# Attention scores from hi/lo pairs, query products over 512 weight columns, and buffer rings of other lengths, in a two-layer transformer kernel

## The chip, the cores and the metric

The kernel runs on one core of a Trainium2 chip, in one launch. The metric is the device time of that launch in microseconds; three runs of the kernel before gave 2274.55, 2277.7 and 2279.82 us, a median of 2277.7 us. Of the core's engines the text speaks of TensorE (PE: matrix products, with weight loads as instructions of their own, PEld), VectorE (DVE), ScalarE (ACT), GpSimd (POOL) and the SyncE queue that issues transfers (SP). Matrix products write to eight PSUM banks of 128 partitions by 512 float32 each; everything else lives in SBUF.

## The reference

Sixteen batches of 64 tokens, width 512, go through two layers. Each sublayer adds its result to x and normalizes over the last axis:

```
x = ln(x + L0_attn(x))      # 32 query heads, 8 kv heads of 128, causal
x = ln(x + L0_xattn(x))     # linear attention over channels, 8 heads of 64
x = ln(x + L0_ffn(x))       # int4 weights with scales, silu(gate) * up, down
x = ln(x + L1_attn(x))      # 32 query heads, 8 kv heads, ALiBi bias
x = ln(x + L1_xattn(x))     # q and k over their rms; keys and values from the context
x = ln(x + L1_ffn(x))       # base plus gated low-rank experts
```

The three softmax attentions share one form, and it is the part that the change is about:

```
q = x @ wq; k, v = src @ wk, src @ wv       # L1_xattn: q = rms(q) * qnw, k = rms(k) * knw
s = (q . k) / sqrt(128) + mask
o = softmax(s) @ v;  out = o @ wo
```

Each kv head serves four query heads (a group). All inputs are float32 and the result is float32.

## The kernel before

A float32 matrix is used on TensorE as a pair hi + lo of fp32r matrices (hi is the value rounded to fp32r, lo the exact rest), and a product is three products, hi*hi + hi*lo + lo*hi, added up in one PSUM bank: `mm3`, lines 101 to 107. The pair is made by a ScalarE copy (hi) and a subtraction (lo), which is VectorE's work where the source lies in PSUM (`split_ps`, lines 91 and 92) and GpSimd's where it lies in SBUF (`split_sb`, lines 86 and 87). Weights come in pieces of 128x512 float32 (256 KB) over the SP queue into tiles `st`, and are split from there.

`Stream` (lines 828 to 1013) runs an attention as steps: one step is one kv head and four batches, 32 steps for a layer, 96 in all. A step has the following parts.

- `scores` (line 847), which is issued two steps ahead, multiplies queries and keys: for each of four batches and two pairs of query heads one product of 128 query rows by 64 keys, straight in float32 (line 856). Both operands are plain float32 tiles: `qt`, the transposed queries of a head and half of the tokens ([hd, 8 batches, 256], 8 KB per partition, two buffers), and `kt`, the transposed keys ([hd, 512], two buffers). Then follow the softmax on VectorE, ScalarE and GpSimd, and the tile `p` with hi and lo of the probabilities side by side.
- `pt` transposes `p` (line 878), `av` multiplies by V (line 889) and splits the result into a tile `ot`, and `oproj` multiplies the previous step's `ot` by the output weights (`mm3`) and adds to x (line 904).
- Between them stand the projections for later heads, in six parts a head (`half_units`, line 817): in the two self attentions `k_unit` and four `q_unit`s, each 12 products of 512 columns into a bank `mm` (of which there are two), evacuated by one ScalarE copy (lines 777 and 788). In the cross attention `qn_front` (line 790) makes the queries of a token tile token-major, with the 128x128 slices of x as the stationary operand, in two groups of 12 products of 256 weight columns each; `rms` divides by the root mean square; `qn_back` transposes (line 807) and copies to `qt` (line 809). The cross attention's keys are loaded by `k_unit` from a scratch tensor `ktd` in DRAM.
- `v_unit` (line 811) computes V of a token tile and `store_v` (line 147) splits it into two tiles `v` and writes them to DRAM; `load_vs` reads them back by batch.

`kv_stream` (line 165) fills `ktd` and the context's V during L0's ffn: `back` transposes the normalized keys into a bank, ScalarE scales them into `pts` (line 186), and one transfer writes them. `q_stream` (line 359) is the queries' side of the linear attention, in chunks of 128 that go through five stages, one a tick (`logits`, `exp`, `norm`, `transpose`, `out`), its work tiles being taken from the tags `s`, `p` and `le`. `l0_ffn` (line 440) keeps the inner activations of two items in one tile `qt`.

The order of instructions on each engine is set by a scheduler when the program is built: it follows the order of the code, moves instructions past each other where one would wait, and takes the softmax and the evacuations marked by `soon` (line 74) early. Buffers are rings by tag, of the lengths in `BUFS` (line 34) and `BANKS` (line 35); a write into a ring's oldest buffer waits for the last reader of it.

## Time and profile before

The profile is of one execution. The page gives its span from the first to the last instruction, 2275.4 us, and no time of its own beside it; the span is 2.3 us below the median of the three timed runs and within their spread.

| what | value |
|---|---|
| median of three runs | 2277.7 us (2274.55 to 2279.82) |
| span of the profiled execution | 2275.4 us |
| PE busy | 2208.5 us (97%), 13200 products |
| PEld busy | 1917.7 us (84%), 13200 loads |
| DVE busy | 1346.0 us (59%), 2523 instructions |
| ACT busy | 1124.1 us (49%), 2195 |
| POOL busy | 1172.9 us (52%), 1001 |
| DMA | 267.24 MB, 117 GB/s on average |
| granted TensorE clock | 0.994 |

Busy times are unions of intervals, so for pipelined products the duration of one (from its start to its modelled end) is longer than the distance to the next; the distance between starts in the timeline is what a product costs in a stream of products. A float32 product that is not a transposition appears as two records (two passes), each with its own weight load; an fp32r product appears as one.

The stages by time: L0 attention from the start to about 750 us, with the linear attention's two sides beside it; L0 ffn, the rest of the linear attention and `kv_stream` to about 1150; L1 self attention to about 1650; L1 cross attention to about 2240; the last L1 ffn tiles to the end.

### The profile page before, as it was taken

The page shows a single profiled execution, that of the slowest core. Times are in us where ns is not written, and L with a number is a line of the kernel's source. Part 1 is how long each engine was busy: PE and PEld are TensorE (multiplying, and loading weights), DVE is VectorE, ACT ScalarE, POOL GpSimd, SP SyncE. Part 2 cuts the span into 40 slices and gives each one's busy share as a digit, 9 for nine tenths or more (in the row PEclk, how much of TensorE's full clock was granted, in tenths as well). Part 3 has the DMA queues.
Part 4 walks back from the last instruction along what each step waited for, and adds up shares of the span by engine and source line. Part 5 has one row for each costly group of instructions (what it writes and reads, how often), then busy time and mean ns, then how long its engine had stood idle before and what let it go on. Part 6 is the DMA issues. An engine that isn't in the chain of part 4 may idle for free.

```text
span 2275.4 us, 36680 instructions
## 1 busy us (share of the span) xinstructions
PE 2208.5 (97%) x13200; PEld 1917.7 (84%) x13200; DVE 1346.0 (59%) x2523; ACT 1124.1 (49%) x2195; POOL 1172.9 (52%) x1001
## 2 busy tenths in 40 slices
PE   8999999999999999999999999999999999999998
PEld 7888888888888777777788888888898899988996
DVE  3655555667645789887743343433356566666656
ACT  5665556555444455555444444444444454443442
POOL 3533334455554655464654554545455666554641
PEclk9999999999999999999999999999999999999999
DMA  7533333322334322456543443334333343332320
GB/s 231 158 115 109 112 105 120 110 84 77 91 114 154 120 83 86 153 180 184 156 144 106 131 126 119 116 111 140 107 113 101 115 123 99 103 105 85 112 70 29
DMA packets 255317, 267.24 MB, mean 117 GB/s; under 512 B 32672, under 2 KB 168352, under 8 KB 255136
## 3 DMA queue, kind: packets, MB, share of 16 engines
q1 hardware_dynamic: 255136, 264.90, 38.1%
q8 instruction: 105, 1.72, 0.3%
q14 instruction: 76, 0.62, 0.1%
HBM read 231.26 MB, written 33.55 MB: 116 GB/s over the span
## 4 chain that ended last, share of the span: by engine, by line
PE 79%; DMA 5%; DVE 5%; POOL 5%; issue 2%; ACT 2%; SPq 0%; POOLq 0%; DVEq 0%; ACTq 0%
PE mm L105 16%; PE mm L106 15%; PE mm L107 15%; PE sc L856 6%; PE o L889 4%; PE fx L105 3%; PE fx L107 3%; PE fx L106 3%; PE pt L878 2%; DMA st<-in_down_s 1%; POOL wo L87 1%; PE fx L325 1%; POOL wq L87 1%; PE fx L298 1%; PE fx L316 1%
## 5 line engine op out<-in xcount | busy, mean ns | idle before, releaser
L87 POOL TENSOR_TENSOR wq<-st,wq 128x512 fp32r<-128x512 f32 x200 | 263.7, 1331 | 329.2 <-ACT wq L86 326.1
L107 PE MATMUL mm<-wo,ot 128*128 128x512 f32 x896 | 352.2, 393 | 0.0
L87 POOL TENSOR_TENSOR wo<-st,wo 128x512 fp32r<-128x512 f32 x226 | 296.6, 1342 | 96.8 <-ACT wo L86 88.0
L105 PE MATMUL mm<-wo,ot 128*128 128x512 f32 x768 | 315.2, 410 | 3.4 <-DVE x L904 3.1
L904 DVE TENSOR_TENSOR x<-x,mm 128x512 f32<-128x512 f32 x192 | 131.1, 683 | 308.2 <-PE mm L107 307.8
L106 PE MATMUL mm<-wo,ot 128*128 128x512 f32 x768 | 301.1, 392 | 0.0
L105 PE MATMUL mm<-xth,wq 128*128 128x512 f32 x512 | 204.9, 400 | 0.6 <-DVE v L92 0.3
L106 PE MATMUL mm<-xtl,wq 128*128 128x512 f32 x512 | 200.9, 392 | 0.0
L107 PE MATMUL mm<-xth,wq 128*128 128x512 f32 x512 | 200.6, 392 | 0.0
L107 PEld LDWEIGHTS mm<-wo,ot 128*128 128x128 f32 x896 | 169.3, 189 | 37.1
L91 ACT CAST ot<-o 128x512 fp32r<-128x512 f32 x192 | 112.3, 585 | 174.6 <-PE o L889 173.6
L114 POOL TENSOR_TENSOR r<-e,nhalf 128x4 f32<-128x4 f32 (+1 forms) x96 | 88.6, 923 | 203.2 <-DVE e L113 194.2
L86 ACT CAST wq<-st 128x512 fp32r<-128x512 f32 x204 | 123.8, 620 | 130.7 <-PE mm L106 73.5
L856 PEld LDWEIGHTS sc<-kt,qt 128*128 128x128 f32 x1536 | 184.4, 193 | 3.1
L856 PE MATMUL sc<-kt,qt 128*128 128x64 f32 x1536 | 185.0, 273 | 0.0
L92 DVE TENSOR_TENSOR ot<-o,ot 128x512 fp32r<-128x512 f32 x192 | 132.0, 687 | 81.8 <-ACT ot L91 81.5
L870 POOL TENSOR_TENSOR s<-s,rc 128x512 f32<-128x512 f32 x96 | 100.6, 1048 | 141.7 <-DVE rc L869 77.4
L105 PEld LDWEIGHTS mm<-wo,ot 128*128 128x128 f32 x768 | 144.6, 188 | 27.9 <-DVE x L904 3.4
L106 PEld LDWEIGHTS mm<-wo,ot 128*128 128x128 f32 x768 | 145.3, 189 | 24.1
L86 ACT CAST wo<-st 128x512 fp32r<-128x512 f32 x226 | 129.7, 624 | 41.0 <-PE mm L106 21.9
L105 PE MATMUL fx<-wq,xth 128*128 128x256 f32 x512 | 149.3, 292 | 0.0
L107 PE MATMUL fx<-wq,xtl 128*128 128x256 f32 x512 | 145.5, 284 | 0.0
(283 smaller groups left out, 5626.1 us busy)
## 6 DMA issues: line engine op xcount, KB each, us to landing
st<-in_wq SPq DMA_DIRECT2D x128, 256.0 KB, 3.1
st<-in_wo SPq DMA_DIRECT2D x128, 256.0 KB, 3.1
vs<-v SPq DMA_DIRECT2D x256, 128.0 KB, 3.1
v<-v SPq DMA_DIRECT2D x128, 128.0 KB, 2.7
st<-in_wqx SPq DMA_DIRECT2D x64, 256.0 KB, 2.9
st<-in_wox SPq DMA_DIRECT2D x64, 256.0 KB, 3.4
vs<-xv SPq DMA_DIRECT2D x128, 128.0 KB, 3.0
st<-in_gu_q SPq DMA_DIRECT2D x56, 256.0 KB, 3.0
```

The costliest lines, as they stand in the source:

```text
L86: self.nc.scalar.copy(hi, src)
L87: (self.nc.vector if fast else self.nc.gpsimd).tensor_tensor(lo, src, hi.bitcast(F32), ALU.subtract)
L91: self.nc.scalar.copy(hi, src)
L92: self.nc.vector.tensor_tensor(lo, src, hi.bitcast(F32), ALU.subtract)
L105: self.nc.tensor.matmul(out, lh, rh, start=first and i == 0, stop=False)
L106: self.nc.tensor.matmul(out, lh, rl, start=False, stop=False)
L107: self.nc.tensor.matmul(out, ll, rh, start=False, stop=last and i == n - 1)
L114: self.nc.gpsimd.tensor_tensor(out, e, self.nhalf[:, :n], ALU.pow)
L856: nc.tensor.matmul(sc[:, i * 64:(i + 1) * 64], qt[:, c + b, gp * 128:(gp + 1) * 128], kt[:, (c + b) * 64:(c + b + 1) * 64], start=True, st ...
L870: nc.gpsimd.tensor_tensor(x, x, rc.unsqueeze(2).to_broadcast([128, 8, 64]), ALU.mult)
L889: nc.tensor.matmul(o[:, b * 256:(b + 1) * 256], self.vs[s][i][:, bp * 2 + b], pts[:, b * 256:(b + 1) * 256], start=i == 0, stop=i == 1)
L904: self.nc.vector.tensor_tensor(n.x[t], n.x[t], ps, ALU.add)
```

## The change

Scores no longer use float32 operands. Queries and keys are kept as fp32r pairs, and each of the eight 64-column score blocks of a step is made by three products (`mm3`) into the same columns. The pairs have to be made: `q_unit` and `k_unit` evacuate by `split_ps` instead of a ScalarE copy, `q_unit` in two pieces of 256 columns because the queries of a head are now four tiles [128, 4, 256] (two quarters of the batches, hi and lo); `qn_back` splits as well; and `back` in `kv_stream` writes hi by ScalarE and lo by VectorE, with two transfers into a scratch tensor that is twice as large.

`qn_front` takes the weights of a head as [k, 512 columns] (the input array is arranged so) and makes 12 products of 512 columns where it made 24 of 256.

The rings have other lengths, and `q_stream` takes its work tiles from three tiles of its own tag `le` (two chunks in each) rather than from `s` and `p`, with its last two stages one tick earlier. Comments are removed throughout.

```diff
-BUFS = {"st": 6, "wq": 6, "wo": 6, "wk": 2, "wv": 2, "v": 4, "vs": 4, "qt": 2, "kt": 2, "s": 3, "p": 3, "pts": 2, "ot": 4}
+BUFS = {"st": 5, "wq": 6, "wo": 6, "wk": 2, "wv": 2, "v": 2, "vs": 4, "qt": 6, "kt": 2, "s": 3, "p": 2, "pts": 2, "ot": 3}
...
-        self.ktd = self.dram.tile([KV, HD, B * S], F32, name="ktd")
+        self.ktd = self.dram.tile([KV, HD, B, 2 * S], F32, name="ktd")
...
-            ks = self.t("pts", [128, 2, 128])
-            nc.scalar.activation(ks, pk, AF.Copy, scale=w)
-            nc.sync.dma_start(self.ktd[2 * hp:2 * hp + 2, :, t * 128:(t + 1) * 128].rearrange("h d t -> d h t"), ks)
+
+            ks = self.t("pts", [128, 4, 128], FR)
+            pb = pk.rearrange("p h (b t) -> p (h b) t", b=2)
+            nc.scalar.activation(ks[:, :, 0:64], pb, AF.Copy, scale=w)
+            nc.vector.scalar_tensor_tensor(ks[:, :, 64:128], pb, w, ks[:, :, 0:64].bitcast(F32), ALU.mult, ALU.subtract)
+            for i in range(2):
+                nc.sync.dma_start(self.ktd[2 * hp + i, :, 2 * t:2 * t + 2], ks[:, 2 * i:2 * i + 2].bitcast(F32))
...
+        ring = [ex.tile([128, 2, 512], F32, name="le", bufs=3) for _ in range(3)]
...
-            s = live[c] = self.t(("s", "p")[c % 2], [128, 8, 64])
+            s = live[c] = ring[c // 2 % 2][:, c % 2].rearrange("p (h d) -> p h d", h=8)
...
-            qh = qhs[c] = ex.tile([128, 4, 128], F32, name="le", bufs=3)
+            qh = qhs[c] = ring[2][:, c % 2].rearrange("p (j n) -> p j n", j=4)
...
-                z2 = ex.tile([128, 8, 64], F32, name="le", bufs=3)
+
+                z2 = self.t("s", [128, 8, 64])
...
-        stages = ((5, out), (4, transpose), (2, norm), (1, exp), (0, logits))
+        stages = ((4, out), (3, transpose), (2, norm), (1, exp), (0, logits))
...
-                pair = self.t("qt", [128, 2, 2, 512], FR)
+                pair = [self.t("qt", [128, 2, 512], FR) for _ in range(2)]
...
     def k_unit(self, half, h):
         n = self.n
-        kt = self.kt[half, h] = n.t("kt", [128, 512])
+        kt = self.kt[half, h] = n.t("kt", [128, 8, 128], FR)
         if self.normed:
-            self.nc.sync.dma_start(kt, self.ktd[h, :, half * 512:(half + 1) * 512])
+            self.nc.sync.dma_start(kt.bitcast(F32), self.ktd[h, :, half * 8:(half + 1) * 8])
             return
...
-        self.nc.scalar.copy(kt, ps)
+        n.split_ps(ps.rearrange("p (b t) -> p b t", b=8), kt[:, :, 0:64], kt[:, :, 64:128])
+
+    def q_tiles(self, half, h):
+
+        self.qt[half, h] = [[self.n.t("qt", [128, 4, 256], FR) for _ in range(2)] for _ in range(2)]
...
-            self.qt[half, h] = n.t("qt", [128, 8, 256])
+            self.q_tiles(half, h)
...
-        self.nc.scalar.copy(self.qt[half, h][:, :, g * 64:(g + 1) * 64], ps.rearrange("p (b q) -> p b q", b=8))
+        for q, qt in enumerate(self.qt[half, h]):
+            n.split_ps(ps[:, q * 256:(q + 1) * 256].rearrange("p (b q) -> p b q", b=4),
+                       *[t[:, :, g * 64:(g + 1) * 64] for t in qt])
...
-        for gp in range(2):
-            w = self.wqs[h, gp]
-            n.mm3(ps[:, gp * 256:(gp + 1) * 256], [n.xt_slices(t, k) + (w[0][:, k], w[1][:, k]) for k in range(4)])
+
+        ws = [[flat(w).rearrange("p (k c) -> p k c", k=2) for w in self.wqs[h, kp]] for kp in range(2)]
+        n.mm3(ps, [n.xt_slices(t, k) + (ws[k // 2][0][:, k % 2], ws[k // 2][1][:, k % 2]) for k in range(4)])
...
-        dst = self.qt[half, h][:, 2 * i:2 * i + 2].rearrange("p b (g q) -> p b g q", g=4)
-        self.nc.scalar.copy(dst, ps.rearrange("p g (b q) -> p b g q", b=2))
+        r = slice(2 * (i % 2), 2 * (i % 2) + 2)
+        n.split_ps(ps.rearrange("p g (b q) -> p b g q", b=2),
+                   *[t[:, r].rearrange("p b (g q) -> p b g q", g=4) for t in self.qt[half, h][i // 2]])
...
-        qt, kt, c = at.qt[half, h], at.kt[half, h], (s % 2) * 4
+        (qh, ql), kt, c = at.qt[half, h][s % 2], at.kt[half, h], (s % 2) * 4
         sc = n.bank("sc")
-        for b in range(4):
-            for gp in range(2):
-                i = b * 2 + gp
-                nc.tensor.matmul(sc[:, i * 64:(i + 1) * 64], qt[:, c + b, gp * 128:(gp + 1) * 128],
-                                 kt[:, (c + b) * 64:(c + b + 1) * 64], start=True, stop=True)
+        for i in range(8):
+            o, b, q = sc[:, i * 64:(i + 1) * 64], i // 2, slice((i % 2) * 128, (i % 2) * 128 + 128)
+            kh, kl = kt[:, c + b, 0:64], kt[:, c + b, 64:128]
+            n.mm3(o, [(qh[:, b, q], ql[:, b, q], kh, kl)])
...
-    for n in ("wq0", "wq1", "wqx"):
+    for n in ("wq0", "wq1"):
         r[n] = r[n].reshape(KV, 2, 128, 1024)
+
+    r["wqx"] = inout(i["L1_xattn_q_proj_w"].T, KV).reshape(KV, 128, 2, 1024).transpose(0, 2, 1, 3)
```

## The prediction

> **What bounds the kernel now.** I read the page's busy shares, granted clock and chain first. Its order of engines and shares:
>
> ```profile
> PE 2208.5 (97%) x13200; PEld 1917.7 (84%) x13200; DVE 1346.0 (59%) x2523; ACT 1124.1 (49%) x2195; POOL 1172.9 (52%) x1001
> ...
> PEclk9999999999999999999999999999999999999999
> ...
> PE 79%; DMA 5%; DVE 5%; POOL 5%; issue 2%; ACT 2%; SPq 0%; POOLq 0%; DVEq 0%; ACTq 0%
> ```
>
> TensorE is busy for 97% of the span at full clock and carries 79% of the chain: only 2275.4 - 2208.5 = 67 us are not PE, some 12 of them at the two ends. Then I read the stages, which hold different work (columns: stretch in us, its length, busy PE, PEld, DVE, ACT, POOL, clock, DMA share, GB/s):
>
> ```profile
> 720.00:900.00 180.00, 162.87 (x858) 130.69 (x858) 149.63 (x290) 89.10 (x165) 98.93 (x86) 0.98 0.32 101
> 900.00:1130.00 230.00, 216.15 (x982) 169.93 (x982) 188.90 (x357) 125.24 (x252) 125.52 (x110) 0.99 0.54 167
> 1130.00:1640.00 510.00, 507.48 (x2886) 439.41 (x2885) 201.36 (x334) 229.06 (x429) 260.42 (x215) 1.00 0.40 123
> 1640.00:2230.00 590.00, 575.20 (x3987) 527.48 (x3985) 358.70 (x626) 272.51 (x516) 341.16 (x289) 0.99 0.34 102
> ```
>
> The attention stages, where all 96 score blocks stand, leave PE almost no idle time: 2.5 us of 510 in L1 attention, 15 of 590 in the cross attention. VectorE is at 39% and 61% there. So PE time added to an attention step is paid in full, and VectorE time added there is mostly covered. Between 720 and 1130 VectorE (83%) and PE (92%) bind together.
>
> What a score product costs is not its duration (273 ns, overlapping its neighbours) but the distance to the next. Two groups by shape, then the timeline of weight loads, then that of products (start, length, engine, line):
>
> ```profile
> L856 PE MATMUL sc<-kt,qt 128*128 128x64 f32 x1536 | 185.0, 273 | 0.0
> ...
> L336 PE MATMUL fx<-ww,lkx 128*128 128x128 f32 x128 | 19.5, 275 | 0.0
> ```
> ```profile
> 209.77 0.53 PEld L336 LDWEIGHTS fx<-ww,lkx 128*128 128x128 f32 x4
> 210.21 0.19 PEld L105 LDWEIGHTS mm<-xth,wk 128*128 128x128 f32 x1
> ...
> 1803.11 1.86 PEld L856 LDWEIGHTS sc<-kt,qt 128*128 128x128 f32 x16
> 1804.89 0.19 PEld L105 LDWEIGHTS fx<-wq,xth 128*128 128x128 f32 x1
> ...
> 1808.14 0.19 PEld L105 LDWEIGHTS mm<-wo,ot 128*128 128x128 f32 x1
> 1808.25 0.19 PEld L106 LDWEIGHTS mm<-wo,ot 128*128 128x128 f32 x1
> ```
> ```profile
> 1803.21 1.90 PE L856 MATMUL sc<-kt,qt 128*128 128x64 f32 x16
> 1804.92 0.36 PE L105 MATMUL fx<-wq,xth 128*128 128x256 f32 x1
> 1805.12 0.28 PE L106 MATMUL fx<-wq,xth 128*128 128x256 f32 x1
> 1805.24 0.28 PE L107 MATMUL fx<-wq,xtl 128*128 128x256 f32 x1
> ...
> 1808.48 0.39 PE L106 MATMUL mm<-wo,ot 128*128 128x512 f32 x1
> 1808.71 0.39 PE L107 MATMUL mm<-wo,ot 128*128 128x512 f32 x1
> ```
>
> A score block is 8 float32 products, recorded as 16 passes (1536 records for 96 x 8 products), each with its own load. It holds PE from 1803.21 to 1804.92, 1.71 us. Sixteen loads take 1804.89 - 1803.11 = 1.78 us, 0.111 each; the four loads of 128-column float32 passes take 210.21 - 209.77 = 0.44, 0.110 each. Half the columns buys nothing: narrow passes are bound by the load. And an fp32r load is no cheaper: two of them stand 1808.25 - 1808.14 = 0.11 us apart, and last 0.19 as the float32 ones do.
>
> **The change, part by part.** Scores. Each block goes from 16 passes to 8 x 3 = 24 fp32r products of 64 columns, each with a load (13200 loads for 13200 products: none is shared now, even where two products in a row have the same stationary tile). Nothing in the trace is an fp32r product this narrow. Nearest row: loads at 0.11 to 0.112, so 8 more at 0.112 = 0.90 us a block, times 96 = **+86 us**, which I take because the load spacing is the same for both types and does not move from 128 to 64 columns. Upper end: the 256-column fp32r products, 1805.24 - 1805.12 = 0.12; 24 x 0.12 - 1.71 = 1.17, x 96 = +112. Lower end of the same mechanism: the block's own 1.71 / 16 = 0.107, 8 x 0.107 = 0.86, x 96 = +82. Further below lies the first rival.
>
> [...] The float32 passes of 128 columns here stand 0.11 apart.
>
> Query front of the cross attention. 16 heads x 4 token tiles = 64 units: 24 products at 0.12 = 2.88 us become 12 of 512 columns at 1808.71 - 1808.48 = 0.23, 2.76; the run of products to the first 512-column one starts alike. With the 0.227 that most such products show, 2.72. I take -0.15 x 64 = **-10** (ends -8 and -13).
>
> Splits of Q and K. VectorE gains 128 `q_unit`s x 2 pieces of 256 columns, 32 `k_unit`s, 64 `qn_back`s and 32 pieces in `kv_stream`:
>
> ```profile
> L91 ACT CAST v<-mm 128x256 fp32r<-128x256 f32 x96 | 35.5, 370 | 70.7 <-PE mm L107 63.0 <-DMA v<-v 5.5 <-DMA st<-in_ctx 2.1
> L788 ACT COPY qt<-mm 128x512 f32<-128x512 f32 x128 | 74.7, 584 | 94.1 <-PE mm L107 94.0
> ...
> L92 DVE TENSOR_TENSOR v<-mm,v 128x256 fp32r<-128x256 f32 x96 | 40.0, 417 | 32.3 <-ACT v L91 29.3 <-DMA vs<-v 1.7
> ```
>
> At 0.417 for 256 and 0.687 for 512 columns: 107 + 22 + 44 + 13 = 186 us, VectorE 1346 to about 1532 (65%); ScalarE +20 (2 x 0.370 for 0.584). What counts is how long the PSUM bank stays held. A `q_unit`'s bank is free after 0.370 + 2 x 0.417 = 1.2 us instead of 0.58; the next user of it comes after `pt`, the 12 products of `oproj` and `av`, over 3 us, so VectorE may lag 2 us. Behind these splits VectorE queues the `ot` split and the add to x, which `oproj` and the other `mm` bank wait for. Cover gone everywhere, the price is 128 x 0.63 + 64 x 0.69 = 125 us; fully covered, 0. VectorE at 39 to 65% in these stages speaks for the low end: **+4**.
>
> Rings. `v` holds one V tile's pair instead of two: the next unit's ScalarE copy waits for the previous transfer (0.34 us to issue, 2.7 to landing, plus the copy, about 3.4 us a unit), and ScalarE's later work queues behind it. In the stream a unit comes once a step (some 14 us or more) and in `kv_stream` every 7 us, so nothing waits. Before each of the two streams four units of 1.44 us stand close together, with score blocks of 2.6 us between them: 0 to 8 us each time, **+4** for both. `qt` (six quarters), `p` (2) and `ot` (3) are refilled after their last reader in PE's own order: 0; `st` 5 for 6 only shortens prefetch of weights that are needed a step later: 0.
>
> `q_stream`. Its own ring frees `s` and `p` for the ffn; PE idled 4.24 us once behind a subtraction into `s`:
>
> ```profile
> 763.95 0.47 PE L105 MATMUL fx<-xth,wq 128*128 128x512 f32 x1 [4.24 <-DVE s L381]
> ```
>
> Against that, a chunk's transposition comes one tick after GpSimd's `norm` (1.05 us behind splits of 1.3) instead of two, and waits in a stage where GpSimd is 55% busy. -8 to +15; **0** taken, the two being alike. The second `ktd` transfer puts 32 issues of 0.38 us on SP and makes them wait for VectorE's lo, with weight loads queued behind: 0 to 12, 0 taken, since PE is not waiting for those loads in the steady part.
>
> Sum: 86 - 10 + 4 + 4 = +84. Against the profiled span 2275.4 + 84 = 2359.4; the median of the runs lies 2.3 above that span, so **2362 us**, 3.7% slower.
>
> **Rivals.** (1) *Narrow fp32r products are not bound by the load.* For: the four fp32r transpositions after 1807.88 start only 0.07 apart, and columns alone would take 0.227 x 64/512 = 0.028. Against: the 0.11 between two ordinary fp32r loads. At 0.05, midway, a block is 1.2 us, -0.51 x 96 = -49, and the time 2275.4 - 49 - 10 + 8 + 2.3 = 2227. It ends faster than before when the spacing is under 0.07 us. Chance 0.05.
>
> (2) *VectorE becomes late.* The longer hold of banks is not covered in L0 attention (64 `q_unit`s, 40 us) and the cross attention (64 x 0.69 = 44 us): 2362 + 84 = 2446, half of it 2404. For: VectorE is at 57 to 62% there before the addition, and cross-attention waits on `pts` and `ot` already make up its 15 idle us. Against: PE was idle for none of the 260 us from 180 to 440 with VectorE at 57%. Chance 0.12 of passing 2395.
>
> (3) *Added score time falls into PE's existing waits.* All 55 idle us between the first and last product, used up, give 2307. Against: most of them lie between 720 and 1130, where no scores are made. Chance 0.03 of under 2335.
>
> **How the numbers follow.** The forecast has 0.80. Low end: 82 - 13 - 8 = +61, 2339, put at 2335 for a little of rival 3; high end: 112 - 8 + 4 + 4, plus 5 of the ring and bank terms, = +117, 2395. The three rivals outside hold 0.2. About 0.2% is what a measurement here can tell from no change; faster 0.04 and same 0.02 come from rival 1 (0.05) and a little from a sum of low ends, slower 0.94.
>
> **What would show it.** Right: 2304 score products (three lines of 768) starting 0.11 apart, a block of about 2.6 us, PE busy near 2285, `qn_front` in 64 x 12 products of 512 columns, VectorE near 1530 busy, PE's idle time within 15 us of before. Wrong: score products under 0.09 apart (rival 1), or idle PE behind VectorE's splits of `qt` (rival 2).

## The result, and the profile after

The changed kernel takes 2464.8 us (2452.6 to 2468.7) against 2278.8 us (2274.6 to 2284.3) of the kernel before on the same chip: ratio 1.081, 95% interval 1.078 to 1.084. It is 186 us slower; the forecast was 84 us slower, and 2465 lies outside the range of 2335 to 2395. The sign was right, the size was less than half.

The page of the kernel after, busy times and granted clock:

```profile
PE 2337.3 (95%) x13200; PEld 1988.6 (81%) x13200; DVE 1514.5 (61%) x2907; ACT 1146.6 (46%) x2323; POOL 1162.6 (47%) x1001
...
PEclk9999999999999999999999999999999999999999
```

The span is 2466.6 us. Span less PE's busy time has gone from 67 to 129 us, so some 62 of the 191 us are new idle time of TensorE. The row of the clock still prints 9 in every slice, and hides something: a digit stands for 62 us. The clock also differs between executions: the four of the changed kernel had a granted clock of 0.977, 0.979, 0.986 and 0.979 on average, at 2468.7, 2465.9, 2452.6 and 2463.6 us; the profile is of the first. The stages by windows tell more. First the kernel before, then the kernel after, each over the same three pieces of work: the L0 ffn (from the 32nd to the 33rd score block), L1 attention (to the 65th), the cross attention (to the 96th). Columns as in the prediction: stretch, length, busy PE, PEld, DVE, ACT, POOL, then granted clock, DMA share, GB/s.

```profile
717.70:1157.00 439.30, 408.05 (x1991) 324.99 (x1990) 355.56 (x674) 227.00 (x440) 247.68 (x215) 0.99 0.44 138
1157.00:1698.90 541.90, 539.65 (x3127) 469.80 (x3126) 213.48 (x350) 244.15 (x458) 269.52 (x222) 1.00 0.40 120
1698.90:2219.90 521.00, 507.28 (x3564) 467.21 (x3562) 325.25 (x571) 240.54 (x458) 307.19 (x262) 0.99 0.34 103
```
```profile
789.00:1254.60 465.60, 421.05 (x1999) 333.75 (x1997) 373.14 (x715) 227.35 (x442) 243.31 (x215) 0.96 0.45 139
1254.60:1852.60 598.00, 577.41 (x3335) 499.36 (x3334) 272.59 (x488) 254.85 (x516) 266.83 (x222) 0.99 0.36 110
1852.60:2409.50 556.90, 535.78 (x3093) 459.80 (x3091) 354.57 (x632) 241.88 (x459) 305.29 (x262) 0.98 0.33 103
```

The L0 ffn, which holds one score block, grew by 26 us: idle time from 31 to 45, and PE busy 13 us longer for nearly the same products (1999 for 1991), at a clock of 0.96 instead of 0.99. L1 attention grew by 56 us; its 32 score blocks were to cost 29. PE idled there 20.6 us where it had idled 2.2.

The score products themselves are as forecast. Two groups by shape, and a block in the timeline of the kernel after:

```profile
L106 PE MATMUL sc<-kt,qt 128*128 128x64 f32 x768 | 215.0, 280 | 0.0
L107 PE MATMUL sc<-kt,qt 128*128 128x64 f32 x768 | 214.9, 280 | 0.0
```
```profile
202.04 0.19 PE L105 MATMUL sc<-kt,qt 128*128 128x64 f32 x1
...
204.42 0.28 PE L106 MATMUL sc<-kt,qt 128*128 128x64 f32 x1
204.53 0.28 PE L107 MATMUL sc<-kt,qt 128*128 128x64 f32 x1
204.64 0.37 PE L105 MATMUL mm<-wv,xth 128*128 128x256 f32 x1
```

24 products from 202.04 to 204.64, 2.60 us, 0.11 apart (204.53 - 204.42); before, 1.71. The median block is 2.60 us over all 96, so 96 x 0.89 = 85 us of the 191 are this.

What TensorE waited for, the first line of the kernel before, then four of the kernel after (engine, tile and line, the releaser: us in total, times, longest):

```profile
PE o L889 <- ACT pts L881: 6.1, 5, 2.5
```

```profile
PE o L899 <- ACT pts L891: 21.9, 21, 3.4
PE mm L105 <- DVE qt L92: 11.5, 8, 3.9
PE fx L403 <- POOL le L397: 6.6, 5, 2.2
PE fx L105 <- DVE le L386: 6.5, 1, 6.5
```

The longest item in both is ScalarE's `pts`, the copy of the transposed probabilities, 16 us more than before; the second, VectorE's lo of the queries, was not among the longest before. Neither holds most of the new idle time. Added up by the engine that came last, TensorE's waits grew from 24 to 51 us behind ScalarE, from 29 to 55 behind VectorE, from 6 to 10 behind GpSimd and from 0 to 4 behind transfers.

The part that the sum had no term for shows when the granted clock is read in windows of 3.4 us. A wait of 2.53 us behind `pts` in L1 attention, then the clock around it, both of the kernel after:

```profile
1452.48 0.74 PE L899 MATMUL o<-pts,vs 128*128 128x256 f32 x4 [2.53 <-ACT pts L891]
```
```profile
1446.60:1450.00 3.40, 3.35 (x18) 2.43 (x16) 0.00 (x0) 1.68 (x3) 1.00 (x1) 1.00 0.45 159
1450.00:1453.40 3.40, 0.92 (x6) 0.88 (x7) 1.28 (x2) 1.82 (x5) 3.40 (x4) 1.00 0.22 77
1453.40:1456.80 3.40, 3.40 (x10) 2.62 (x9) 0.69 (x1) 0.44 (x1) 1.60 (x2) 0.50 0.43 141
1456.80:1460.20 3.40, 3.40 (x19) 2.81 (x18) 0.85 (x2) 1.24 (x3) 0.00 (x0) 1.00 0.04 13
```

After the wait the clock is 0.50 for one stretch of 3.4 us, which has 10 products instead of 18 or 19. In it two products of 512 columns start 0.43 us apart (at 1454.05 and 1454.48) and last 0.63 us; behind it two start 0.23 apart (at 1456.93 and 1457.16) and last 0.40 and 0.39. Adding up all stretches of the trace whose granted clock is a half: 28 us in the kernel before (7 stretches), 114 us in the kernel after (23). If work at half the rate takes twice as long (0.43 for 0.23 us comes near it), 86 more such us cost about 43; this is an estimate, and the forced gaps below put the price a little lower, at 0.4 to 0.5 us for each.

So the span's +191 is about 85 of score products, -10 of the query front, 62 of idle time and 43 at half rate, which leaves about 11 that I assign to nothing (up to 20 at the lower price). The forecast held the first two.

### The profile page after: what moved, and what is told of

It is laid out like the page before. It is cut to its first block, busy times and chain, and to the rows that moved or that the text cites. A ratio compares the mean times of both kernels' runs of the same rounds, so it can differ in the third digit from the quotient of the medians.

```text
span 2466.6 us, 37413 instructions
## 1 busy us (share of the span) xinstructions
PE 2337.3 (95%) x13200; PEld 1988.6 (81%) x13200; DVE 1514.5 (61%) x2907; ACT 1146.6 (46%) x2323; POOL 1162.6 (47%) x1001
## 5 line engine op out<-in xcount | busy, mean ns | idle before, releaser
L87 POOL TENSOR_TENSOR wo<-st,wo 128x512 fp32r<-128x512 f32 x226 | 288.8, 1306 | 92.0 <-ACT wo L86 91.2
L92 DVE TENSOR_TENSOR qt<-mm,qt 128x256 fp32r<-128x256 f32 x256 | 108.0, 422 | 252.9 <-ACT qt L91 252.4
L105 PE MATMUL mm<-xth,wq 128*128 128x512 f32 x512 | 209.4, 409 | 16.3 <-DVE qt L92 10.3
L106 PE MATMUL sc<-kt,qt 128*128 128x64 f32 x768 | 215.0, 280 | 0.0
L107 PE MATMUL sc<-kt,qt 128*128 128x64 f32 x768 | 214.9, 280 | 0.0
L105 PE MATMUL sc<-kt,qt 128*128 128x64 f32 x768 | 208.5, 271 | 0.0
L107 PE MATMUL mm<-xth,wq 128*128 128x512 f32 x512 | 203.4, 397 | 0.0
L899 PEld LDWEIGHTS o<-pts,vs 128*128 128x128 f32 x768 | 114.3, 189 | 58.4 <-ACT pts L891 42.9
```

What stands on the lines that cost most here:

```text
L87: (self.nc.vector if fast else self.nc.gpsimd).tensor_tensor(lo, src, hi.bitcast(F32), ALU.subtract)
L92: self.nc.vector.tensor_tensor(lo, src, hi.bitcast(F32), ALU.subtract)
L105: self.nc.tensor.matmul(out, lh, rh, start=first and i == 0, stop=False)
L106: self.nc.tensor.matmul(out, lh, rl, start=False, stop=False)
L107: self.nc.tensor.matmul(out, ll, rh, start=False, stop=last and i == n - 1)
L899: nc.tensor.matmul(o[:, b * 256:(b + 1) * 256], self.vs[s][i][:, bp * 2 + b], pts[:, b * 256:(b + 1) * 256], start=i == 0, stop=i == 1)
```

## The experiments

Differences are to the kernel before as it ran beside each on the same chip, 2278 to 2280 us. Idle time is the sum of all gaps between a product's modelled end and the next product; half-rate time is the sum of the stretches granted half the clock. The account of each profiled span, in us, with half of the added half-rate time as its price. Each row is one execution, and that of `a_hi` is the fastest of its four, at a granted clock of 0.994 where the others had 0.986 to 0.991:

| run | span, change | products and front | idle | half rate, added time / 2 | sum |
|---|---|---|---|---|---|
| the changed kernel | +191 | 75 | 62 | 43 | 180 |
| a_two | +87 | -10 | 64 | 22 | 76 |
| a_hi | +116 | 75 | 26 | 2 | 103 |
| a_hi_s | +155 | 75 | 46 | 24 | 145 |
| b_prod | +116 | 85 | 16 | 14 | 115 |
| b_rings | +72 | 0 | 44 | 26 | 70 |
| b_rq | +42 | 0 | 34 | 8 | 42 |
| b_qstream | +13 | 0 | 11 | 4 | 15 |
| b_p2 | +31 | 0 | 23 | 9 | 32 |
| b_st5 | +32 | 0 | 24 | 2 | 26 |
| b_v2 | +13 | 0 | 9 | 5 | 14 |
| b_front | -10 | -10 | 1 | -3 | -12 |

The account closes within about 6 us for changes made to the kernel before, and misses 10 to 13 us in each kernel that has the pairs.

**One part alone on the kernel before: the rings, the front.**

```diff
-BUFS = {"st": 6, "wq": 6, "wo": 6, "wk": 2, "wv": 2, "v": 4, "vs": 4, "qt": 2, "kt": 2, "s": 3, "p": 3, "pts": 2, "ot": 4}
+BUFS = {"st": 5, "wq": 6, "wo": 6, "wk": 2, "wv": 2, "v": 2, "vs": 4, "qt": 2, "kt": 2, "s": 3, "p": 2, "pts": 2, "ot": 3}
```

> The kernel before with only the shorter rings: st 5 for 6, v 2 for 4, p 2 for 3, ot 3 for 4 (qt stays two of the old tiles). Theory 'rings' (the shorter rings make ScalarE and TensorE wait, which is most of the 105 us that the result lies above the forecast): 40 to 100 us slower than before, with ScalarE waiting for weight loads. Theory 'order on ScalarE' (the query evacuation, cut in two, is what holds the banks): within 10 us of before. The forecast itself put the rings at +4.

Measured 2347.2 us (2340.5 to 2349.1), ratio 1.029 (1.027 to 1.031), +67. The four ring lengths, costed at 4 us in the forecast, cost 67 by themselves. 46 of them fall into the L0 ffn, 10 into the cross attention, 7 ahead of the 5th score block.

The front alone is this, and `wqx` arranged to fit:

```diff
-        for gp in range(2):
-            w = self.wqs[h, gp]
-            n.mm3(ps[:, gp * 256:(gp + 1) * 256], [n.xt_slices(t, k) + (w[0][:, k], w[1][:, k]) for k in range(4)])
+        ws = [[flat(w).rearrange("p (k c) -> p k c", k=2) for w in self.wqs[h, kp]] for kp in range(2)]
+        n.mm3(ps, [n.xt_slices(t, k) + (ws[k // 2][0][:, k % 2], ws[k // 2][1][:, k % 2]) for k in range(4)])
```

> The kernel before with only the cross attention's query front as 12 products of 512 weight columns. By the distance between product starts (0.12 for 256, 0.227 for 512 columns): 64 x 0.15 = 10 us faster than before, about 2268, all of it in the cross-attention stage. If the stage is held by VectorE or ScalarE instead of TensorE: no change.

Measured 2268.4 us (2265.6 to 2270.0), ratio 0.995 (0.993 to 0.997): -11.5 us, 10.7 of it in the cross attention, where the queries are made. This term held, and the part alone is faster than both kernels.

**In the changed kernel: one product fewer, and the order of two copies.** `a_two`:

```diff
-            n.mm3(o, [(qh[:, b, q], ql[:, b, q], kh, kl)])
+            nc.tensor.matmul(o, qh[:, b, q], kh, start=True, stop=False)
+            nc.tensor.matmul(o, ql[:, b, q], kh, start=False, stop=True)
```

> The changed kernel with two products a score block instead of three (the third, query hi times key lo, is left out, so the scores are less exact; all splits are still made). By the load price, 8 x 0.112 x 96 = 86 us faster than the changed kernel, about 2379, and what is left over before is splits, rings and order: +100. If part of the added score time stood in TensorE's waits, less than 86 comes back: 2395 to 2440.

Measured 2363.8 us (2359.6 to 2367.3), ratio 1.037 (1.035 to 1.039). The third product is worth 101 us, 16 more than its spacing says, and what is left is still 84 us over the kernel before although each block has its 16 loads back. So the products are not the whole excess.

For `a_adj`, the reason is in the timeline of the kernel after. In a `q_unit`, ScalarE writes hi of the first 256 columns, VectorE subtracts, and then the second hi copy stands in ScalarE's queue behind a cast of `p` that waits for GpSimd (start, length, engine and line; idle before it and its releaser in brackets):

```profile
1315.81 0.39 PE L107 MATMUL mm<-xth,wq 128*128 128x512 f32 x1
1316.24 0.38 ACT L91 CAST qt<-mm 128x256 fp32r<-128x256 f32 x1
1317.17 0.38 DVE L92 TENSOR_TENSOR qt<-mm,qt 128x256 fp32r<-128x256 f32 x1
1319.37 0.62 ACT L86 CAST p<-s 128x512 fp32r<-128x512 f32 x1 [2.19 <-POOL s L880]
1319.89 0.37 ACT L91 CAST qt<-mm 128x256 fp32r<-128x256 f32 x1
1320.29 0.42 DVE L92 TENSOR_TENSOR qt<-mm,qt 128x256 fp32r<-128x256 f32 x1 [2.75 <-ACT qt L91]
1320.86 0.47 PE L105 MATMUL mm<-xth,wq 128*128 128x512 f32 x1 [1.10 <-DVE qt L92]
```

The bank, full at 1316.2, is free at 1320.7: 4.5 us where the forecast reckoned 1.2, and PE waits 1.10. VectorE is not busy in it; it idles 2.75 us for ScalarE. The edit puts both hi copies together, then both subtractions, and marks them `soon`:

```diff
-        for q, qt in enumerate(self.qt[half, h]):
-            n.split_ps(ps[:, q * 256:(q + 1) * 256].rearrange("p (b q) -> p b q", b=4),
-                       *[t[:, :, g * 64:(g + 1) * 64] for t in qt])
+        src = [ps[:, q * 256:(q + 1) * 256].rearrange("p (b q) -> p b q", b=4) for q in range(2)]
+        hl = [[t[:, :, g * 64:(g + 1) * 64] for t in qt] for qt in self.qt[half, h]]
+        with n.soon():
+            for q in range(2):
+                self.nc.scalar.copy(hl[q][0], src[q])
+            for q in range(2):
+                self.nc.vector.tensor_tensor(hl[q][1], src[q], hl[q][0].bitcast(F32), ALU.subtract)
```

> The changed kernel with the two ScalarE copies of a query unit issued next to each other, then the two VectorE subtractions, all marked to be taken early. Theory 'order on ScalarE': the bank is free 1 to 3 us sooner, the idle time of TensorE before the query and key products goes, and with it part of the half-clock stretches: 30 to 50 us faster than the changed kernel, 2415 to 2435. Theory 'rings': within 10 us of 2465.

Measured 2453.0 us (2446.2 to 2460.6), ratio 1.075 (1.072 to 1.078), 12 us (0.5%) off the changed kernel's. L1 attention's excess falls from 56 to 48 us. Over all 128 units of the kernel after, the bank is held 2.0 us in the median (1.7 to 7.3, more than 4 us in 15 of them), so the place above is one of the long ones; in `a_adj` it is 1.8 us. The gain of 12 us is at the edge of the noise, since the runs of the two kernels overlap. The wait is real, but this order is a small part at most; the theory that expected 30 to 50 us of it falls.

**q_stream and the rings together.** `b_rings` charges the short rings to a kernel whose `q_stream` still takes from `s` and `p`; the change frees these. `b_rq` is both, `b_qstream` the second alone:

```diff
-            s = live[c] = self.t(("s", "p")[c % 2], [128, 8, 64])
+            s = live[c] = ring[c // 2 % 2][:, c % 2].rearrange("p (h d) -> p h d", h=8)
...
-        stages = ((5, out), (4, transpose), (2, norm), (1, exp), (0, logits))
+        stages = ((4, out), (3, transpose), (2, norm), (1, exp), (0, logits))
```

> The kernel before with the four shorter rings and with q_stream's own ring and its two stages a tick earlier; no pairs, no new scores, no new query front. Theory A (the 46 us that the rings alone cost in the ffn stage came from q_stream's chunks, which shared the rings of s and p with the ffn; their own ring gives that back): about 20 to 30 us over the kernel before, 2300 to 2310. Theory B (the ffn's excess of the changed kernel comes from the ffn's own use of p and st, so q_stream's ring returns only the difference between 46 and the 26 that the changed kernel shows): about +47, 2325. Theory C (the stages a tick earlier cost by themselves): over +60, above 2340.

> The kernel before with only q_stream's own ring and its two earlier stages. The forecast had 0 (-8 to +15), that is 2272 to 2295. If freeing s and p takes the waits behind subtractions into s out of the ffn stage: -5 to -10, 2270 to 2275. If a transposition that comes one tick after GpSimd's norm makes TensorE wait: +10 to +25, 2290 to 2305, with waits on q_stream's lines at the ffn stage.

`b_rq`: 2320.2 us (2318.5 to 2323.4), ratio 1.017 (1.016 to 1.019), +40; the ffn stage holds 23 of it. `b_qstream`: 2290.1 us (2289.5 to 2295.3), ratio 1.005 (1.003 to 1.006), +10, 14 in the ffn stage. Both edits cost something alone, and the second takes 27 us off the first. Theory B is the nearest for `b_rq`, whose ffn stage keeps about what the changed kernel's has in excess (26); theory A, which gave all of it back, falls.

`b_ring` leaves the stages where they were (no edit of the last two lines) and gives the chunks their own tiles:

> The kernel before with q_stream's own ring alone; its stages stay where they were. Run together with the stages, this part of the change cost 10 us, 14 of them in the ffn stage. If the stages did that (a transposition close behind GpSimd's norm): the ring alone gives -5 to +2. If the ring did (le, which the chunks' norms and queries go through, has fewer places): +8 to +15.

Measured 2282.4 us (2278.3 to 2286.0), ratio 1.0022 (1.0011 to 1.0033), +4. The earlier stages then account for about the other 6 of the 10 us; the split is finer than either theory had it.

**The lo part of the queries, with long and short rings.** Both runs use `qh` where the changed kernel has `ql`, so all 24 products remain but the third repeats the first, and there is no subtraction in `q_unit` and `qn_back`; `a_hi` also has `st` 6, `v` 4, `p` 3 (the memory comes from the tiles of lo):

```diff
-            n.split_ps(ps[:, q * 256:(q + 1) * 256].rearrange("p (b q) -> p b q", b=4),
-                       *[t[:, :, g * 64:(g + 1) * 64] for t in qt])
+            self.nc.scalar.copy(qt[:, :, g * 64:(g + 1) * 64], ps[:, q * 256:(q + 1) * 256].rearrange("p (b q) -> p b q", b=4))
...
-            n.mm3(o, [(qh[:, b, q], ql[:, b, q], kh, kl)])
+            n.mm3(o, [(qh[:, b, q], qh[:, b, q], kh, kl)])
```

> The changed kernel without the lo part of the queries: the hi part stands in its place in the second product, so all 2304 products stay and the scores are less exact; VectorE loses the subtractions of q_unit and qn_back, and the memory that this frees gives st, v and p their old lengths (6, 4, 3; ot stays 3). If the excess over the forecast came from these subtractions and the short rings: the terms of products and query front alone, +86 - 10, and a little for ot, K's split and q_stream, 2350 to 2375, with half-rate time under 50 us. If it came from the products themselves, from K's pair and its second transfer, or from q_stream: 2400 to 2450.

> The same without the lo part of the queries, but with the short rings of the changed kernel. The distance to the run with long rings is what the rings cost in the changed kernel, the distance to the changed kernel what the subtractions of the queries cost. Rings the main cause: 2420 to 2450. Subtractions the main cause: 2360 to 2385. Rings as dear as on the kernel before (+67) and the rest the subtractions: about 2420.

`a_hi`: 2400.5 us (2393.1 to 2403.1), ratio 1.052 (1.050 to 1.054), +120. `a_hi_s`: 2431.6 us (2420.6 to 2436.8), ratio 1.065 (1.062 to 1.069), +152. So in the changed kernel the rings are worth 31 us and the subtractions of the queries 34 (186 - 152), about alike. Of the 34, 16 are idle time and 19 half rate, by the account above. (The third product as it stands here makes the scores about twice as large; the instructions are of the same kind and number.) But 120 us remain in `a_hi`, where the forecast's products and front give 76: its second expectation, with the cause in the products, the keys or `q_stream`. The next run says which.

**The products alone.** `b_prod` makes the 24 products on the kernel before, from the rounded q and k (the copies that are there write fp32r), with nothing else of the change; the scores come out about three times too large:

```diff
-                nc.tensor.matmul(sc[:, i * 64:(i + 1) * 64], qt[:, c + b, gp * 128:(gp + 1) * 128],
-                                 kt[:, (c + b) * 64:(c + b + 1) * 64], start=True, stop=True)
+                q, k = qt[:, c + b, gp * 128:(gp + 1) * 128], kt[:, (c + b) * 64:(c + b + 1) * 64]
+                n.mm3(sc[:, i * 64:(i + 1) * 64], [(q, q, k, k)])
```

> The kernel before with the scores as 24 fp32r products of 64 columns a block, taken from the rounded q and k alone (written as fp32r by the copies that are there already; the scores come out some three times too large): no subtraction, no second transfer, no shorter ring, no q_stream, no new front. It prices the products by themselves. Forecast's term: +86 (82 to 112), 2362 to 2366. If what the removal of a third product gave back (101 us) is the products' own price, 24 to 16: 2380. If the products cost less and the rest lies in what feeds them: under 2355.

Measured 2392.3 us (2386.5 to 2397.7), ratio 1.050 (1.048 to 1.053), +115, more than any theory had. The block is 2.60 us here too, so the spacing is worth 85 us; 16 more are idle time and 14 half rate. The longest item of its waits, the same one as in the changed kernel:

```profile
PE o L889 <- ACT pts L881: 15.7, 10, 3.1
```

It was 6.1 us before. That the longer block itself moves the softmax against the rest of a step is not shown: the scheduler also made another order. In the two profiles 398 of ScalarE's 2195 instructions and 182 of VectorE's 2523 stand at another place in the order (compared by operation, tiles and shapes), against 6 and 7 for `b_front`, whose cost came out as forecast. The two were not separated.

Now the parts come near the whole: products +115, rings with `q_stream` +40, subtractions of the queries +34, front -11.5, together +178 of 186. The pair of the keys, the second `ktd` transfer and the parts' effects on each other are in the other 8; these were not separated. The parts were measured in different kernels, three on the kernel before and one in the changed one, so effects on each other can hide in the sum as well.

**The rings one by one, on the kernel before.** `b_p2` has `p` 2 for 3, `b_v2` `v` 2 for 4, `b_st5` `st` 5 for 6, each alone.

```diff
-BUFS = {"st": 6, "wq": 6, "wo": 6, "wk": 2, "wv": 2, "v": 4, "vs": 4, "qt": 2, "kt": 2, "s": 3, "p": 3, "pts": 2, "ot": 4}
+BUFS = {"st": 5, "wq": 6, "wo": 6, "wk": 2, "wv": 2, "v": 4, "vs": 4, "qt": 2, "kt": 2, "s": 3, "p": 3, "pts": 2, "ot": 4}
```

(`b_st5`; the others likewise.)

> The kernel before with the ring p of 2 tiles for 3, nothing else. The forecast had 0. Theory A (p, shared by softmax, the ffn's partial sums and q_stream, is the dear one of the four): +35 to +50, mostly in the ffn stage. Theory B (st is): under +10.

> The kernel before with the ring v of 2 tiles for 4, nothing else. The forecast had +4 (0 to 16), at the start of the two streams, 2280 to 2296. If ScalarE's copies behind the transfers of v hold up softmax in the cross attention too: +15 to +25.

> The kernel before with the ring st of 5 tiles for 6, nothing else. The forecast had 0. If the ring is dear in the ffn, where int weights, their scaled copies and weight pieces all go through it: +10 to +30. If prefetch has a step to spare as the forecast says: within 5 of the kernel before.

| run | us | ratio (95%) | change | where |
|---|---|---|---|---|
| b_p2 | 2310.1 (2308.4 to 2316.2) | 1.015 (1.013 to 1.017) | +32 | ffn 33 |
| b_st5 | 2308.9 (2306.8 to 2313.2) | 1.014 (1.012 to 1.016) | +31 | ffn 15, cross attention 10 |
| b_v2 | 2289.1 (2288.7 to 2290.5) | 1.005 (1.004 to 1.007) | +11 | start 5, ffn 5 |

Theories A and B were both too simple: `p` and `st` are equally dear. The three add up to 74 us, where all four lengths together cost 67. `p` was forecast by its reader in the attention, "PE's own order". But the ffn and `q_stream` take from it too, and the waits of `b_p2` put `q_stream`'s transposition behind a subtraction into the shared tiles, an item that is not among the longest of the kernel before:

```profile
PE fx L398 <- DVE s L381: 12.2, 4, 4.2
PE fx L105 <- DVE s L381: 6.7, 2, 5.4
```

For `st` the waits of TensorE in `b_st5` name no transfer at all; the longest item is `pts`, 16.2 us in 14 times, 10 of the 24 us of added idle time. A place in its cross attention:

```profile
1893.19 0.46 PE L878 MATMUL pt<-identr,p 128*128 128x128 f32 x4
1893.47 0.63 ACT L86 CAST wo<-st 128x512 fp32r<-128x512 f32 x1
1895.16 1.36 DVE L866 TENSOR_TENSOR s<-s,mx 128x512 f32<-128x512 f32 x1
1896.62 0.63 ACT L867 ACTIVATE s<-s 128x512 f32<-128x512 f32 x1 [2.52 <-DVE s L866]
1897.63 0.58 ACT L881 CAST pts<-pt 128x512 fp32r<-128x512 f32 x1
```

The transposition is done at 1893.65, the copy to `pts` starts at 1897.63, because ScalarE stands 2.52 us at the next step's exponential, which is queued ahead of it and waits for VectorE. (The kernel before has this order too, at 1860 us for one, with a wait of 1.42 us.) A ring length changes not only when a buffer comes free, but the order that the scheduler makes. In the profile of `b_st5`, 289 of ScalarE's 2195 instructions, 111 of VectorE's 2523 and 109 of GpSimd's 1001 stand at another place in the order than in the kernel before; in that of `b_p2` 144, 231 and 39; in that of `b_v2`, the cheapest of the three, 109, 31 and 3. How much of the time is the new order and how much the later refill was not separated. With `ot` 3 for 4 the scheduler builds the same order on all five engines, with one more wait on ScalarE; that length was not run alone.

**Forced gaps: does idle time bring the half rate?** `b_gap4` makes the eighth product of each L1 score block take its keys from a copy which VectorE makes after four other copies, and holds later products behind it:

```diff
+                if at.alibi is not None and i == 7:
+                    with n.soon():
+                        x = n.t("s", [128, 8, 64])
+                        for _ in range(4):
+                            nc.vector.tensor_copy(flat(x)[:, 64:512], sc[:, 0:448])
+                        nc.vector.tensor_copy(x[:, 7], k)
+                    k = x[:, 7]
```

`b_gap2` has two such copies, `b_gap1` one of 64 columns.

> The kernel before with one short forced wait of TensorE in each of the 32 score blocks of L1 attention, a stage in which it idled 2 us of 542: the eighth product takes its keys from a copy that VectorE makes after a copy of 64 columns of the first seven products' scores, and the products behind it are held in place. Results and rings unchanged. Wait some 0.6 to 1.2 us each, by VectorE's rows for so little: +20 to +40 in the stage. Theory H (idle time of about 2 us and more is what brings the half-rate stretches): no half-rate stretch in the stage, so the stage grows by its idle time alone. Rival (any idle time brings them, or they come with the load of the chip): some there, too.

> The same with two copies of 448 columns in front, 0.5 to 0.7 us each by VectorE's rows of that size, so a wait of 1.5 to 2.2 us, +48 to +70 of idle time. Theory H: a part of the 32 waits is followed by a half-rate stretch (32 of 70 gaps between 1.5 and 2 us were, over the ten traces at hand), each 3.4 us long or a multiple, at a price of some 1.7 us: +10 to +40 more. Rival: no more than the idle time.

> The same with four copies of 448 columns, a wait of 2.5 to 3.5 us, +80 to +110 of idle time. Theory H: nearly every one of the 32 is followed by 3.4 or 6.8 us at half rate (68 of 76 gaps of 2 us and more were), at 1.7 to 3.4 us each: +50 to +110 more, the kernel near 2430 to 2480. Rival: idle time alone, 2360 to 2390.

| run | us | change | L1 stage | idle added there | half-rate time there | gaps of 2 us and more | followed by half rate |
|---|---|---|---|---|---|---|---|
| b_gap1 | 2351.1 (2347.3 to 2354.9) | +73 | +74 | 49 | 41 | 1 | 1 |
| b_gap2 | 2399.1 (2392.9 to 2404.4) | +121 | +122 | 72 | 102 | 18 | 18 |
| b_gap4 | 2444.0 (2441.4 to 2445.2) | +166 | +166 | 105 | 133 | 32 | 32 |

In the kernel before this stage had no half-rate stretch. One of the 32 places of `b_gap4`, as wait and in windows:

```profile
1443.95 0.43 PE L871 MATMUL sc<-s,qt 128*128 128x64 f32 x2 [2.99 <-DVE s L869]
```
```profile
1437.60:1441.00 3.40, 3.37 (x23) 2.91 (x21) 0.46 (x1) 1.62 (x3) 1.04 (x1) 1.00 0.53 154
1441.00:1444.40 3.40, 0.45 (x3) 0.45 (x4) 2.69 (x5) 0.00 (x0) 1.46 (x2) 1.00 0.39 139
1444.40:1447.80 3.40, 3.40 (x15) 3.21 (x15) 2.49 (x4) 0.85 (x2) 0.00 (x0) 0.50 0.04 16
1447.80:1451.20 3.40, 3.40 (x18) 2.79 (x18) 0.89 (x2) 1.04 (x3) 1.05 (x1) 0.99 0.23 77
```

It is the picture of the changed kernel at 1450. The waits came out longer than expected for `b_gap1` (1.6 to 2.0 us, not 0.6 to 1.2) and `b_gap2` (up to 3.3 us, not 2.2), so no run has really short gaps, and that these bring no half rate was not put to the test; 9 of the 24 gaps of `b_gap1` between 1.5 and 2 us were followed by half rate. TensorE's idle time is the cause: where waits were put in, the stretches came, after each of the 51 gaps of 2 us and more. The price follows as well. In `b_gap4` the stage grew by 166 us, of which 105 are idle; the other 61 over 133 us at half rate are 0.46 us for each; in `b_gap2` (122 - 72) / 102 = 0.49, in `b_gap1` (74 - 49) / 41 = 0.61. The ratio is highest where there is least half rate, so some of it belongs to the inserted waits themselves; from `b_gap1` to `b_gap4` alone it is (92 - 56) / 92 = 0.39. The rival, idle time alone, is excluded by the 61 and 50 us.

**Towards a faster kernel.** Two runs add rings to the front alone, with `ot` 3 to make room: `f_p4` has `p` 4, `f_st7` has `st` 7 and `s` 4.

```diff
-BUFS = {"st": 6, "wq": 6, "wo": 6, "wk": 2, "wv": 2, "v": 4, "vs": 4, "qt": 2, "kt": 2, "s": 3, "p": 3, "pts": 2, "ot": 4}
+BUFS = {"st": 6, "wq": 6, "wo": 6, "wk": 2, "wv": 2, "v": 4, "vs": 4, "qt": 2, "kt": 2, "s": 3, "p": 4, "pts": 2, "ot": 3}
```

> The kernel before with the new query front, a ring p of 4 for 3 and, to make room, ot of 3 for 4. The front alone gave -11.5. If a longer p gives back some of what a shorter one costs (32 us) and the fourth ot is idle: -15 to -25, 2253 to 2263. If ot's fourth tile was needed or p's third is enough: -12 to +10.

> The same with the room of the fourth ot given to st (7 for 6) and s (4 for 3). A longer st and s would shorten the waits behind weights and behind subtractions into s, 5 us of which end in the longest gap of the ffn stage: -15 to -25. If these waits come from the engines and not from the rings: within 5 of the front alone, 2265 to 2272.

`f_p4`: 2264.7 us (2261.8 to 2267.3), ratio 0.993 (0.992 to 0.995), 15 us faster than the kernel before and the fastest kernel here. Its interval overlaps that of the front alone, so whether the fourth `p` gives anything is open. `f_st7`: 2297.3 us (2292.8 to 2297.7), ratio 1.007 (1.006 to 1.009), 18 us slower, outside what either theory had: 44 us of idle time in the ffn stage for 35 with the front alone, and 20 for 12 in the cross attention. `ot` 3 is in both runs and cannot be the reason for the difference between them. Five tiles of `st` cost 31 us against six, and seven, with a fourth `s`, cost time too (which of the two does, was not separated): the lengths are not a scale on which more is better.

## Why the prediction was wrong, point by point

- **Scores, +86.** The spacing was right: 0.11 between products, 2.60 us a block, 85 us. The step "PE time added to an attention step is paid in full, and VectorE time added there is mostly covered" was only half right. Alone, the longer blocks cost 115 us: on top of the 85 come 16 of idle time and 14 at half rate.
- **Query front, -10.** Right: -11.5 alone.
- **Splits of Q and K, +4 (0 to 125).** Mis-sized; the queries' part alone is 34 us. The step that failed is "a `q_unit`'s bank is free after 0.370 + 2 x 0.417 = 1.2 us": it adds durations and leaves out the queue. In the changed kernel no unit had its bank back before 1.7 us, the median was 2.0, and where the second hi copy stood behind another wait of ScalarE it was 4.5 us. VectorE's load was forecast well (1514.5 us for 1532), and it was not what mattered; bringing the two copies together gave back some 12 us, near the noise.
- **Rings, +4.** The largest wrong step, though not by far: 36 us short with `q_stream`'s tiles, where the scores were 29 and the splits 30 short. Alone on the kernel before they cost 67 us; with `q_stream`'s own tiles 40; in the changed kernel without lo of the queries 31. `p`, forecast at 0, is worth 32 and `st`, forecast at 0, 31; `v`, forecast at 4, is worth 11, all three on the kernel before, whose `q_stream` still takes from `p`. Each ring was judged by one reader, in a fixed order of instructions; but several stages share a ring, and the scheduler makes a new order for each length. `ot` at 0 agrees with the unchanged order, but was not run alone.
- **q_stream, 0 (-8 to +15).** +10 alone, within its bounds, and -27 beside the short rings.
- **The second `ktd` transfer, 0.** Not separated; at most some part of the 8 us that are left over.
- **No term for the clock.** The profile before showed a wait of 4.24 us at 759.7, and behind it, from 764.4 to 767.8, a granted clock of 0.50, with 10 products in these 3.4 us; the sum used only the mean, 0.994. About 35 to 43 us of the result is the price of half-rate time.
- **The range.** Its high end gave 5 us to the ring and bank terms beyond their taken values, where the prediction itself bounds the splits at 125, the rings at 16, `q_stream` at 15 and the second transfer at 12 us. The range did not carry these bounds.
- **Rivals.** Rival 1 (narrow products not bound by the load) falls with the 0.11. Rival 3 (the added time falls into idle time) falls: idle time grew. Rival 2 (VectorE late, 2404 to 2446) is nearest in size, and its sign in the profile is there: 11.5 us of waits behind VectorE's splits of the queries and 4.0 behind those of the keys, a quarter of the added idle time. In the place shown above VectorE was not busy but idle for ScalarE, so it is late there by the order of ScalarE and not by its load.
- **What would show it.** Score spacing, block, `qn_front` in 12 products of 512 columns and VectorE's busy time came as written. "PE's idle time within 15 us of before" failed by 47 us, and PE's busy time (2337 for 2285) failed, for the most part by the half rate (about 43 of the 52 us, by the estimate above), since it counts the slower products as longer: 0.63 for 0.40 us at the place shown above.

## What to carry to other kernels

Cost a shorter ring by everything that takes from it, and by the order that the scheduler builds for it, which can be compared before a run (the one part whose order stayed, the query front, cost what its products said); "refilled after its last reader" is no argument where the order itself is made anew. On an engine that is 97% busy, price new idle time with what follows it: here 0.4 to 0.5 us for each us at half rate, which came in stretches of 3.4 us and more. Where a bank is emptied in several pieces, reckon the hold from the queue of the engine that empties it, not from the durations.

## What the runs showed of the hardware

Half-rate stretches came in lengths of 3.4 us and its multiples (71 of 3.4, 32 of 6.8 and 4 of 10.2 us in ten traces, those of the two kernels and of eight runs without forced gaps, the first and last 60 us of each left aside), and 99 of these 107 began within 6 us of the start of a TensorE gap of 1.5 us or more. By length of the gap: 68 of 76 gaps of 2 us and more were followed by one within 6 us, 32 of 70 between 1.5 and 2, 26 of 415 between 0.5 and 1.5. In the forced runs all 51 of 2 us and more were, in the stage with the forced waits.

Another count separates the cases better than the length of the gap. In each trace all half-rate stretches (but one cut short at the very end) begin and end on one grid of 3.413 us. Counted by the windows of this grid, in all 20 traces with the first and last 60 us left aside: of the windows at full rate in which TensorE's idle time added up to 2.0 us or more, 142 of 142 were followed by a window at half rate; with 1.8 to 2.0 us 40 of 43; with 1.6 to 1.8 us 18 of 64; with less, 28 of 12477. So in these traces 2.0 us of idle time within one window were always followed by half rate, while a long gap across a boundary could pass: all 8 gaps of 2 us and more in the ten traces above that had no half rate behind them lay across one. The longest of them, in `a_adj`, as wait and in windows of the grid:

```profile
1894.46 0.74 PE L903 MATMUL o<-pts,vs 128*128 128x256 f32 x4 [3.34 <-ACT pts L895]
```
```profile
1889.43:1892.85 3.42, 1.69 (x8) 1.07 (x6) 3.23 (x4) 0.03 (x1) 0.96 (x1) 1.00 0.88 289
1892.85:1896.26 3.41, 1.80 (x12) 1.67 (x13) 2.07 (x4) 2.71 (x6) 1.71 (x2) 1.00 0.10 36
1896.26:1899.67 3.41, 2.91 (x16) 2.32 (x15) 1.83 (x4) 2.03 (x4) 2.79 (x3) 1.00 0.23 77
```

TensorE idled for 1.7 us of the first window and 1.6 of the second, and the clock stayed full. The grid does not begin with the program: its first boundary lies 3.19 us after the first instruction in the trace of the kernel before and 2.72 in that of the kernel after. Whether this is also why the granted clock differs between executions of one kernel is not shown, with one trace for each.
